# Attention block and 7x7 depthwise convolution on one core: how the rows for TensorE's share of the convolution are loaded, where a test of sums stands, and where the last additions go

## The chip, the cores and the metric

The kernel runs on one core of one Trainium2 chip. The metric is the device time of one execution in microseconds (us). A profile of one execution accompanies it; in it PE is TensorE, PEld its weight loads, DVE VectorE, ACT ScalarE, POOL GpSimd and SP SyncE. A "q" after an engine's name (SPq, ACTq) marks the engine's instruction queue where it issues a DMA or waits.

## The reference

The input `x` is (16, 384, 32, 32): 16 images of 384 channels and 32x32 positions, all float32.

```python
# _gn: normalised over 32 groups of 12 channels and all positions (mean, variance, eps 1e-5)
# layer 0
qkv  = einsum('bnc,oc->bno', tokens(_gn(x)), w_qkv)            # 8 heads of 48
attn = softmax(einsum('bhnd,bhmd->bhnm', q, k) * 48 ** -0.5)   # 1024 x 1024 per head
o    = einsum('bhnm,bhmd->bhnd', attn, v)
x    = x + einsum('bnc,oc->bno', o, w_proj) + b_proj
# layer 1
w_sym = (w + rot90(w, 1) + rot90(w, 2) + rot90(w, 3)) * 0.25   # one 7x7 filter per channel
x    = x + depthwise_conv(_gn(x), w_sym, stride 1, pad 3)
```

## The kernel before

The kernel goes through the images one after another. For image `b` it makes q, k and v, the scores and the attention (`s_step`, `av_step`), and the projection; TensorE does all of that, and ScalarE the exponentials between. Channels stand on the 128 partitions, so an image is three tiles of 128 channels by 1024 positions; `(b, k)` below is tile `k` of image `b`. The convolution of image `b - 1` runs on VectorE meanwhile, as a list of operations made by `fold_ops` and taken one at a time by `tap()`: sums and differences of a padded copy (`side`, L733), weighted sums of rows (`rows_e`, `rows_o`, L736 and L739), and additions to the output tile (L746). A planner decides at build time where each of these stands: it keeps two clocks of estimated times (`clock`, `vclock`), a heap `later` filled by `after(wait, cost, f)`, and `applies` for ScalarE's work. On the chip every engine then runs its list strictly in order, and semaphores are all that ties the lists together.

Three tiles at the end, `PE_TILES` = (14, 2), (15, 2) and (15, 1), have their convolution on TensorE instead. The last tile, (15, 0), stays with VectorE. The way of a TensorE tile is:

- `conv_begin` normalises it into `xn`, and `conv_store` (L895) writes that to a buffer `xd` in the chip's main memory, split by row parity into two planes per channel, each with a margin of zero rows.
- `conv_load` (L910) reads it back for half a tile (`a` = 0, 1) into a buffer `sh` of 128 partitions by 4 groups of 512 positions. A partition of `sh` stands for one channel of 16 and one of eight row shifts; a group is another 16 channels. The rows overlap, so each half tile comes to 1 MB.
- `conv_on_pe` (L941) multiplies `sh` with matrices made from the filter (`conv_matrices`, from `wsh` and `eye`, both filled by `conv_prepare`): 7 column shifts by 4 groups, 28 matrix products per half tile, each recorded as two. `pe_conv` holds the pieces to be done; `conv_piece` does one and calls `loads` for more rows.
- `conv_take` (L956) copies the sums out of PSUM on ScalarE, `conv_perm` (L965) sorts their rows on TensorE, and `conv_add` (L980) adds the result to the tile on VectorE and stores it (L981).

Main-memory loads that are issued by one engine wait in its list for earlier ones: the program has eight semaphores for the DMAs of SP and ACT together, and a DMA that takes a semaphore waits until that one's last DMA has landed.

The end of the program is written out by hand in `fast_finish` and `fast_end`: last projection, statistics of image 15 (`groups_on_pe`, from L325 to L357), then the tail. In it SP issues the stores, `late["tail"]` splits the row loads between SP and ACT, and a loop drains what is left. A safety test belongs there too: `check_vector` (L1363 to L1370) reduces the softmax sums, `check_tensor` (L1376 to L1379) adds the findings over the partitions and writes `again`, by which a slower exact version would be run. PSUM buffers are taken in turn from two pools.

```python
RI, CG = KS + 1, P // (KS + 1)      # 8 row shifts, 16 channels to a group
NG = P // CG                        # 8 groups in a tile, 4 in a half
PLANE = (H // 2 + PAD) * W          # 608 numbers: one row parity of one channel
```

Of the kernel before, what the change touches and what calls it, by code (L numbers as in the profile page):

```python
# [10 lines left out]
F32 = mybir.dt.float32  # L11
I32 = mybir.dt.int32
AF = mybir.ActivationFunctionType
ALU = mybir.AluOpType
AX = mybir.AxisListType

P = 128
# [28 lines left out]
def kernel(  # L46
# [25 lines left out]
    nc = tc.nc  # L72

    B, C, H, W = x.shape
    N = H * W
# [44 lines left out]
    def run(general):  # L120
        tag = "g" if general else "f"
        with ExitStack() as stack:
# [697 lines left out]

            def conv_end(b, k):

                (nc.scalar if b == B - 1 and not general else nc.gpsimd).dma_start(  # L823
                    out[b, k * P : (k + 1) * P].rearrange("p h w -> p (h w)"), x1s.pop((b, k))
                )

# [5 lines left out]
            RI, CG = KS + 1, P // (KS + 1)  # L832
            NG = P // CG
            PLANE = (H // 2 + PAD) * W

            def conv_prepare():

                w_d = dconv.tile([C, (KS + 2) * KS], F32, tag="w", name="w_d")
                zero = tpool.tile([P, N], F32, tag="t", name="zero")[:, 0 : 2 * W]
                nc.gpsimd.memset(zero, 0.0)  # L840
                w_rows = w_d.rearrange("(k p) t -> p k t", p=P)
                with nc.allow_non_contiguous_dma(reason="small, once"):
                    nc.gpsimd.dma_start(
                        w_rows[:, :, KS : (KS + 1) * KS], wsym.rearrange("p k i j -> p k (i j)")
                    )
                    none = zero[:, 0 : NK * KS].rearrange("p (k t) -> p k t", k=NK)
                    nc.gpsimd.dma_start(w_rows[:, :, 0:KS], none)
                    nc.gpsimd.dma_start(w_rows[:, :, (KS + 1) * KS :], none)
                    for n, k in enumerate(PE_K):
                        for i in range(RI):  # L850
                            nc.gpsimd.dma_start(
                                wsh[CG * i : CG * (i + 1), n].rearrange("p g t d -> p g (t d)"),
                                bass.AP(
                                    w_d.tensor,
                                    w_d.offset + (k * P * (KS + 2) + i) * KS,
                                    [[(KS + 2) * KS, CG], [CG * (KS + 2) * KS, NG], [1, 2 * KS]],
                                ),
                            )
                for bk in PE_TILES:
                    xd = dconv.tile([P, 2 * PLANE], F32, tag=f"x_{len(xds)}", name=f"xd_{len(xds)}")  # L860
                    xds[bk] = xd

                    for lo, n in ((0, 1), (H // 2 + 1, 2), (H // 2 + 3, 2), (2 * PLANE // W - 1, 1)):
                        nc.gpsimd.dma_start(xd[:, lo * W : (lo + n) * W], zero[:, 0 : n * W])
                for q in range(RI):
                    src = ident[:, CG * q : CG * (q + 1)]
                    if q == 0:
                        nc.gpsimd.tensor_copy(eye, src)
                    else:
                        nc.gpsimd.tensor_tensor(eye, eye, src, ALU.add)  # L870
                for row in range(2):
                    nc.gpsimd.tensor_copy(
                        perm[:, row].rearrange("p (g c) -> p g c", c=CG),
                        ident.rearrange("p (g t c) -> p t g c", t=2, c=CG)[:, 1 - row],
                    )
# [28 lines left out]
            def conv_load(b, k, a):  # L904

                t = qkpool.tile([P, 2, N], F32, tag="qk", name=f"sh_{b}_{k}_{a}")
                t = t.rearrange("p a n -> p (a n)").rearrange("p (g n) -> p g n", n=HALF)
                xd = xds[b, k]
                for i in range(RI):
                    (nc.scalar if late.get("tail") and i % 2 else nc.sync).dma_start(  # L910
                        t[CG * i : CG * (i + 1)],
                        bass.AP(
                            xd.tensor,
                            xd.offset
                            + a * NG // 2 * CG * 2 * PLANE
                            + (0 if i % 2 else PLANE)
                            + i // 2 * W,
                            [[2 * PLANE, CG], [CG * 2 * PLANE, NG // 2], [1, HALF]],
                        ),
                    )  # L920
                shs[b, k, a] = t
# [36 lines left out]
            def conv_perm(b, k, a):  # L958

                nonlocal clock  # L960
                if (b, k) not in pss:
                    pss[b, k] = psum(f"ps_rows_{b}_{k}")
                part = slice(64 * a, 64 * a + 64)
                for row in range(2):
                    nc.tensor.matmul(  # L965
                        pss[b, k][part, row, :],
                        lhsT=perm[:, row],
                        rhs=shs[b, k][:, a, :],
                        start=True,
                        stop=True,  # L970
                    )
                clock += 2.2
                if (b, k) == PE_TILES[-1]:
                    after(0.5, 1.3, lambda: conv_add(b, k, part, (nc.scalar, nc.sync)[a]))
                elif a == 1:
                    after(3.5 if b < B - 1 else 0.5, 1.3, lambda: conv_add(b, k, slice(0, P), nc.gpsimd))

            def conv_add(b, k, part, queue):
                dst = by_rows(x1s[b, k][part])
                nc.vector.tensor_tensor(dst, grids(pss[b, k][part]), dst, ALU.add)  # L980
                queue.dma_start(  # L981
                    out[b, k * P + part.start : k * P + part.stop].rearrange("p h w -> p (h w)"),
                    x1s[b, k][part],
                )
# [100 lines left out]
            def after(wait, cost, f):  # L1085

                nonlocal count
                count += 1
                heapq.heappush(later, (now() + wait, count, cost, f))
# [280 lines left out]
                nc.vector.memset(ones, 1.0)  # L1370
                lims.append((ones, lim))

            def check_tensor(pair):
                ones, lim = pair
                ps = psum("ps_again")
                nc.tensor.matmul(ps[0:1, 0, 0:2], lhsT=ones, rhs=lim, start=True, stop=True)  # L1376
                good = small.tile([1, 1], F32, tag="good", name="good")
                nc.vector.tensor_reduce(good, ps[0:1, 0, 0:2], AX.X, ALU.add)
                nc.vector.tensor_scalar(again, good, -1.0, 2.0 * P, ALU.mult, ALU.add)  # L1379
# [60 lines left out]
            def fast_finish(b):  # L1440
                nonlocal clock, vclock
                late["tail"] = b == B - 1

                for o in range(NK):
                    proj_part(b, o, 1, (0, 1))
                    if o < 2:
                        divide_at_once(o)
                    if o == 0:
                        tap()
                conv_piece()  # L1450
                for t in (2, 3):
                    for o in range(NK):
                        proj_part(b, o, 1, (t,))
                for o in range(NK):
                    half_done(b, o, 1)
                    if o == 0:
                        x1_stats[b].first_channels(x1s[b, o])
                clock += 2 * US_PROJ + 1.0
                vclock = clock + 2.5

            def fast_end(b):
                nonlocal clock, vclock
                assert not applies
                x1_stats[b].groups_on_pe(late["masks"], tap, lambda: conv_piece(False))
                conv_piece(False)
                x1_chains(b, x1_stats[b])
                clock = now()
                vclock = clock + 1.0
                after(0.0, 1.2, check_vector)
                heapq.heappop(applies)[-1]()  # L1470
                loads(2)
                clock += 3.0
                heapq.heappop(applies)[-1]()
                conv_rows()
                clock += 4.5

            def once(key, when):
                if when and key not in late:
# [63 lines left out]
            fast_end(B - 1)  # L1542
            while later or state["done"] < len(order) or active or pe_conv or perms:
                if pe_conv:
                    if pe_conv[0][0] == B - 1 and lims:
                        check_tensor(lims.pop())
                    conv_piece()
                elif perms:
                    conv_rows()
                else:  # L1550
                    clock = now() + 1.0
                act_slot(9.0)
                catch_up(clock)
# [51 lines left out]
```

## Time and profile before

| | us |
|---|---|
| median of 3 runs | 2870.86 (2870.76 to 2872.58) |
| the profiled execution, its own time | 2872.72 |
| its span, first to last instruction | 2870.9 |
| PE busy | 2832.4 (99%) |
| DVE busy | 2083.9 (73%) |
| ACT busy | 1649.1 (57%) |
| POOL busy | 250.6 (9%) |

The span is what the profile explains; 1.8 us of the execution's time lie around it. The shares are means over stages with different limits: the last 75 us of the span, after the statistics of image 15, have another pattern than the 2,795 us before. In a timeline row the first two numbers are the start from the span's beginning and the duration, "xN" is the number of instructions merged in the row, and the brackets hold the engine's idle time before it and what ended that. In the chain of waits a row is a piece of the chain that ended last.

### The profile page before, as it was taken

The page shows a single profiled execution, that of the slowest core. Times are in us where ns is not written, and L with a number is a line of the kernel's source. Part 1 is how long each engine was busy: PE and PEld are TensorE (multiplying, and loading weights), DVE is VectorE, ACT ScalarE, POOL GpSimd, SP SyncE. Part 2 cuts the span into 40 slices and gives each one's busy share as a digit, 9 for nine tenths or more (in the row PEclk, how much of TensorE's full clock was granted, in tenths as well). Part 3 has the DMA queues.
Part 4 walks back from the last instruction along what each step waited for, and adds up shares of the span by engine and source line. Part 5 has one row for each costly group of instructions (what it writes and reads, how often), then busy time and mean ns, then how long its engine had stood idle before and what let it go on. Part 6 is the DMA issues. An engine that isn't in the chain of part 4 may idle for free.

```text
span 2870.9 us, 46047 instructions
## 1 busy us (share of the span) xinstructions
PE 2832.4 (99%) x19342; PEld 1115.2 (39%) x19342; DVE 2083.9 (73%) x2257; ACT 1649.1 (57%) x1925; POOL 250.6 (9%) x410
## 2 busy tenths in 40 slices
PE   9999999999999999999999999999999999999995
PEld 5344343433434344343433434344343433434331
DVE  4502968959597695968959597695968959597776
ACT  2637647475674747647475674747647375674730
POOL 3201012210101001010010101001010010101000
PEclk9999999999999999999999999999999999999998
DMA  6612131211212112130211212112130211212215
GB/s 239 189 37 49 32 75 29 53 49 44 63 33 62 45 37 64 32 75 24 50 50 44 63 33 62 45 37 63 32 75 24 50 50 44 64 33 60 78 39 103
DMA packets 75657, 167.35 MB, mean 58 GB/s; under 512 B 31952, under 2 KB 34000, under 8 KB 73904
## 3 DMA queue, kind: packets, MB, share of 16 engines
q0 software_dynamic: 32400, 107.53, 14.3%
q1 hardware_dynamic: 41536, 54.16, 7.5%
q10 hardware_dynamic: 1504, 2.62, 0.6%
q8 instruction: 154, 2.52, 0.4%
q14 instruction: 63, 0.52, 0.1%
HBM read 117.09 MB, written 28.68 MB: 51 GB/s over the span
## 4 chain that ended last, share of the span: by engine, by line
PE 95%; DVE 3%; DMA 1%; issue 1%; ACT 0%; ACTq 0%; POOL 0%; SPq 0%; DVEq 0%; POOLq 0%
PE ps_s L518 30%; PE acc L538 30%; PE ps_qk L447 17%; PE ps_v L473 9%; PE ps_proj L599 8%; DVE x L746 1%; DVE rows_e L736 1%; DMA sh<-xd 1%; PE warm L1325 0%; DVE side L733 0%; DMA inv<-rec 0%; DMA inv<-inv 0%; DVE rows_o L736 0%; DVE x L736 0%; DVE x L980 0%
## 5 line engine op out<-in xcount | busy, mean ns | idle before, releaser
L526 ACT ACTIVATE e<-ps_s 128x1024 f32<-128x1024 f32 x1024 | 1021.2, 1030 | 448.1 <-PE ps_s L518 447.4
L538 PE MATMUL acc<-e,v 64*64 64x512 f32 x8192 | 1040.5, 588 | 0.6 <-ACT o L551 0.6
L518 PE MATMUL ps_s<-qk 48*64 48x512 f32 x8192 | 1040.8, 589 | 0.0
L733 DVE TENSOR_TENSOR side<-padded 128x1024 f32<-128x1024 f32 x270 | 329.0, 1219 | 345.5 <-ACT padded L704 345.5
L736 DVE SCALAR_TENSOR_TENSOR rows_e<-side,even,rows_e 128x1024 f32<-128x1024 f32 x405 | 509.6, 1274 | 85.6 <-ACT rows_e L715 84.0
L538 PEld LDWEIGHTS acc<-e,v 64*64 64x64 f32 x8192 | 308.8, 132 | 575.8 <-issue 574.2
L518 PEld LDWEIGHTS ps_s<-qk 48*64 48x64 f32 x8192 | 307.5, 132 | 577.4 <-issue 525.8
L447 PE MATMUL ps_qk<-x,wqk 128*128 128x512 f32 x1152 | 502.8, 595 | 0.0
L447 PEld LDWEIGHTS ps_qk<-x,wqk 128*128 128x128 f32 x1152 | 218.2, 191 | 278.0 <-issue 272.4
L746 DVE TENSOR_TENSOR x<-x,rows_o 128x992 f32<-128x992 f32 (+3 forms) x271 | 309.8, 1144 | 3.0
L746 DVE TENSOR_TENSOR x<-x,rows_e 128x992 f32<-128x992 f32 (+2 forms) x270 | 310.8, 1151 | 0.0
L454 ACT COPY qk<-ps_qk 128x1024 f32<-128x1024 f32 x96 | 97.2, 1012 | 319.4 <-PE ps_qk L447 319.4
L473 PE MATMUL ps_v<-wv,x 128*128 128x384 f32 x768 | 252.6, 486 | 0.0
L599 PE MATMUL ps_proj<-o,wp 128*128 128x512 f32 x540 | 234.2, 592 | 0.0
L493 ACT COPY v<-ps_v 64x384 f32<-64x384 f32 x256 | 121.4, 474 | 122.5 <-PE ps_v L473 120.0
L473 PEld LDWEIGHTS ps_v<-wv,x 128*128 128x128 f32 x768 | 145.9, 190 | 108.2 <-issue 14.3
L736 DVE SCALAR_TENSOR_TENSOR rows_o<-side,odd,rows_o 128x1024 f32<-128x1024 f32 x135 | 172.8, 1280 | 1.6
L736 DVE SCALAR_TENSOR_TENSOR x<-side,even,x 128x1024 f32<-128x1024 f32 x135 | 172.5, 1278 | 0.0
L823 POOL DMA_DIRECT2D out<-x x44 | 24.8, 563 | 1600.3 <-DVE x L746 1599.8
L715 ACT ACTIVATE rows_e<-padded,even 128x1024 f32<-128x1024 f32 x135 | 146.7, 1166 | 11.0 <-DMA sh<-xd 11.0
L599 PEld LDWEIGHTS ps_proj<-o,wp 128*128 128x128 f32 x540 | 102.6, 190 | 126.2 <-issue 117.4
L607 ACT ACTIVATE x<-ps_proj,bp 128x1024 f32<-128x1024 f32 x45 | 50.1, 1114 | 167.6 <-PE ps_proj L599 167.6
(145 smaller groups left out, 1013.1 us busy)
## 6 DMA issues: line engine op xcount, KB each, us to landing
x<-in_x POOLq DMA_DIRECT2D x90, 512.0 KB, 5.5
inv<-inv SPq DMA_DIRECT2D x126, 256.0 KB
out<-x POOLq DMA_DIRECT2D x46, 512.0 KB, 3.0
xs<-in_x POOLq DMA_DIRECT2D x42, 512.0 KB, 6.4
qk<-qk POOLq DMA_DIRECT2D x96, 128.0 KB, 4.1
o<-o SPq DMA_DIRECT2D x180, 32.0 KB
sh<-xd SPq DMA_DIRECT2D x32, 128.0 KB
x<-in_x SPq DMA_DIRECT2D x6, 512.0 KB
```

What stands on the lines that cost most here:

```text
L447: nc.tensor.matmul(ps[:, h, :], lhsT=wqk[:, k, s, t, :], rhs=xns[b][:, k, h * HALF : (h + 1) * HALF], start=(k == 0), stop=(k == NK - 1),)
L454: nc.scalar.copy(halves(qks[u][:, s, :]), ps)
L473: nc.tensor.matmul(ps[:, j, 0:C], lhsT=xns[b][:, k, t * P : (t + 1) * P], rhs=wv[:, k, :], start=(k == 0), stop=(k == NK - 1),)
L493: nc.scalar.copy(dst[:, :, 0 : HEADS // 2 * (D + 1)].rearrange("p k (h d) -> p k h d", d=D + 1)[:, :, :, 0:D], src.rearrange("p k (h d) -> ...
L518: nc.tensor.matmul(ps[64 * c : 64 * c + 64, a, :], lhsT=qk[r, 1, 64 * kb : 64 * kb + 64], rhs=qk[r, 0, h * HALF : (h + 1) * HALF], start=True,
L526: nc.scalar.activation(es[n], ps, AF.Exp, scale=SCALE)
L538: nc.tensor.matmul(accs[a][64 * j : 64 * j + 64, :], lhsT=v[rows, kb, c : c + 64], rhs=e[rows, j, :], start=(kb == 0), stop=(kb == 2 * NT ...
L599: nc.tensor.matmul(ps[:, h, :], lhsT=wp[:, t, o * P : (o + 1) * P], rhs=os_[b, t // 2][:, t % 2, h * HALF : (h + 1) * HALF], start=(t == 0 ...
L715: nc.scalar.activation(grid(rows_e[dy - 1]), padded_view(i), AF.Identity, scale=even[:, k, dy, 0:1],)
L733: vec.tensor_tensor(grid(sides[n]), padded_view(i, j), padded_view(i, -j), op)
L736: vec.scalar_tensor_tensor(dst, src, w, dst, ALU.mult, ALU.add)
L746: vec.tensor_tensor(dst, dst, src[:, lo + dy * W : hi + dy * W], op)
```

## The change

- **Row loads.** `conv_load` issues 4 DMAs per half tile, one per group, each to all 128 partitions of that group; before it was 8, one per row shift, each to 16 partitions and all four groups. The partitions are numbered with the channel outermost and the shift innermost. All are issued by SP. `wsh` and `eye` are filled in the same numbering by a new function `inputs`.
- **Test of the sums.** `check_vector` is called in `fast_finish`, ahead of the last part of the projection; `check_tensor` keeps only the matrix product and is called in the middle of the statistics, ahead of a convolution piece; the two small VectorE operations become `check_end`, called once the statistics are applied.
- **Additions.** Tiles (14, 2) and (15, 2) are no longer added by VectorE: ScalarE copies the sorted rows to a buffer `conv`, and POOL issues a DMA that adds the buffer to the tile, and then the store. The two half additions of (15, 1) are put 13.0 us of planner time later.
- **Order in `fast_end`.** The copies `conv_take` of (14, 2) come ahead of `rows_e`, `conv_perm` after it.

```diff
             def conv_end(b, k):
-                (nc.scalar if b == B - 1 and not general else nc.gpsimd).dma_start(
+                nc.gpsimd.dma_start(
...
+            def inputs(i):
+                first = (1 - i % 2) * RI // 2 + i // 2
+                return slice(first, first + (CG - 1) * RI + 1, RI)
             def conv_prepare():
...
-                                wsh[CG * i : CG * (i + 1), n].rearrange("p g t d -> p g (t d)"),
+                                wsh[inputs(i), n].rearrange("p g t d -> p g (t d)"),
...
-                    src = ident[:, CG * q : CG * (q + 1)]
+                    src = ident[:, inputs(q)]
...
             def conv_load(b, k, a):
...
-                for i in range(RI):
-                    (nc.scalar if late.get("tail") and i % 2 else nc.sync).dma_start(
-                        t[CG * i : CG * (i + 1)],
+                for i in range(NG // 2):
+                    nc.sync.dma_start(
+                        t[:, i],
                         bass.AP(
                             xd.tensor,
-                            xd.offset
-                            + a * NG // 2 * CG * 2 * PLANE
-                            + (0 if i % 2 else PLANE)
-                            + i // 2 * W,
-                            [[2 * PLANE, CG], [CG * 2 * PLANE, NG // 2], [1, HALF]],
+                            xd.offset + (a * NG // 2 + i) * CG * 2 * PLANE,
+                            [[PLANE, 2 * CG], [W, RI // 2], [1, HALF]],
                         ),
                     )
...
             def conv_perm(b, k, a):
...
                 if (b, k) == PE_TILES[-1]:
-                    after(0.5, 1.3, lambda: conv_add(b, k, part, (nc.scalar, nc.sync)[a]))
+                    after(13.0, 1.3, lambda: conv_add(b, k, part, (nc.scalar, nc.sync)[a]))
                 elif a == 1:
-                    after(3.5 if b < B - 1 else 0.5, 1.3, lambda: conv_add(b, k, slice(0, P), nc.gpsimd))
+                    t = tpool.tile([P, N], F32, tag="t", name=f"conv_{b}_{k}")
+                    nc.scalar.copy(by_rows(t), grids(pss.pop((b, k))))
+                    nc.gpsimd.dma_start(x1s[b, k], t, accum_op=ALU.add)
+                    conv_end(b, k)
...
-            def check_tensor(pair):
-                ones, lim = pair
+            def check_tensor():
+                ones, lim = lims.pop()
                 ps = psum("ps_again")
                 nc.tensor.matmul(ps[0:1, 0, 0:2], lhsT=ones, rhs=lim, start=True, stop=True)
+                lims.append(ps)
+
+            def check_end():
+                ps = lims.pop()
                 good = small.tile([1, 1], F32, tag="good", name="good")
...
             def fast_finish(b):
...
+                check_vector()
                 conv_piece()
...
             def fast_end(b):
...
-                x1_stats[b].groups_on_pe(late["masks"], tap, lambda: conv_piece(False))
+                x1_stats[b].groups_on_pe(
+                    late["masks"], tap, lambda: (check_tensor(), conv_piece(False))
+                )
                 conv_piece(False)
                 x1_chains(b, x1_stats[b])
                 clock = now()
                 vclock = clock + 1.0
-                after(0.0, 1.2, check_vector)
+                check_end()
                 heapq.heappop(applies)[-1]()
                 loads(2)
+                for p in perms:
+                    conv_take(*p)
+                heapq.heappop(applies)[-1]()
+                while perms:
+                    conv_perm(*perms.popleft())
                 clock += 3.0
-                heapq.heappop(applies)[-1]()
-                conv_rows()
-                clock += 4.5
...
-                    if pe_conv[0][0] == B - 1 and lims:
-                        check_tensor(lims.pop())
```

## The prediction

> **What bounds the kernel now.** I read the page's shares first. PE is busy for 99% of the span, so up to the end of the last projection nothing but TensorE's own work counts; none of that work is changed. The chain of waits over the last 75 us tells another story:
>
> ```profile
> 2797.27 0.81 DVE xn L363
> ...
> 2798.11 2.83 DMA xd<-xn
> ...
> 2802.47 7.83 DMA sh<-xd
> ...
> 2810.69 3.23 ACT rows_e L715 x3
> 2813.92 0.48 ACT rows L956
> ...
> 2814.53 4.08 PE ps_rows L965 x8
> ...
> 2818.63 1.23 DVE x L980
> ```
>
> The statistics are ready at 2797.2, and VectorE begins the convolution of (15, 0), the list that ends the program, only at 2819.8. Its first entry is the addition for (14, 2), which waits for PE's row sorting, which waits for ACT's copies, which stand behind row loads that ACT issues. ACT's timeline and the waits of this stretch show the queue:
>
> ```profile
> 2801.12 9.52 ACTq L910 DMA_DIRECT2D sh<-xd  x8
> 2810.69 3.23 ACT L715 ACTIVATE rows_e<-padded,even 128x1024 f32<-128x1024 f32 x3 [11.03 <-DMA sh<-xd]
> ```
> ```profile
> DVE x L980 <- PE ps_rows L965: 19.5, 1, 19.5
> PE ps_rows L965 <- ACT rows L956: 15.9, 3, 14.5
> ```
>
> ACT issues eight loads but is held 9.52 us, because it has to wait for earlier ones to land. Why they are slow is seen in a table of stretches (last columns: PE clock, DMA share, GB/s):
>
> ```profile
> 2799.00:2802.00 3.00, 1.05 (x12) 0.13 (x4) 0.12 (x2) 0.66 (x1) 0.00 (x0) 1.00 0.93 350
> 2812.00:2826.00 14.00, 11.47 (x82) 3.66 (x82) 7.33 (x9) 2.87 (x4) 0.59 (x1) 0.75 1.07 129
> ```
>
> The stores from 128 partitions move 350 GB/s at 0.93 busy; the loads to 16 partitions move 129 GB/s at full business. From 2819.8 to 2865.2 VectorE never stops. PE's row of work for (15, 2) and (15, 1) runs beside it:
>
> ```profile
> 2818.53 6.12 PE L941 MATMUL ps_conv<-sh,mat 128*32 128x512 f32 x56
> ...
> 2849.26 1.93 PE L965 MATMUL ps_rows<-rows,perm 128*64 128x512 f32 x4 [0.70 <-ACT rows L956]
> ```
>
> That is 32.7 us from 2818.53 to 2851.19, two waits of 0.7 for ACT's copies included. The last store is issued at 2865.20 and the span ends 5.7 us later. So the tail is: 22 us of waiting, 45.4 us of VectorE, 5.7 us of store.
>
> **What the Trainium skill says.** "SBUF — State Buffer", section "Door 1: The DMA port swizzle", states that the rate of a transfer follows the ports that its partitions reach: 104 GB/s measured for partitions 0 to 15, 328 for 0 to 127, at 1 MiB. The trace agrees in kind with 129 and 350; two queues that load different sixteens may explain why 129 is above 104. "DMA: Bandwidth & Descriptors", section "Issuing engines are not separate DMA queues", states that issuing from a second engine saves only the sequencer's time. In this trace it costs ACT 9.5 us of waiting.
>
> **Part by part.** Times are those of the profiled span.
>
> *Row loads.* In the tail 32 loads of 128 KB become 16 of 256 KB, all on SP, none on ACT: ACT loses three blocks of 9.5, 3.8 and 2.0 us. SP needs 0.30 to 0.64 us for an issue, so four take about 2 us and carry 1.05 MB, faster than the data flow; behind them on SP stand only the next loads and, far later, stores. The first can go at 2801.09 as before, since it waits for the store of (15, 2), landed at 2800.94. That store took 2.83 us for 0.52 MB, of which 1.5 is data at 350, so some 1.3 us pass before data flow (an estimate). At the skill's 328 GB/s, close to the trace's 350, half a tile takes 3.2 us: the first half of (15, 2) is in at 2801.1 + 1.3 + 3.2 = 2805.6, the other three at 2808.8, 2812 and 2815.2. PE wants them at 2812 or later, so they are hidden. The rate is the unknown here. From below it is the present 129 to 135 (all 4.2 MB by 2833), from above 350.
> For (14, 2), at 2715 to 2734, 16 issues on SP become 8, so VectorE's 8.9 us of idle time there, for reciprocals that SP sends behind the loads, shrinks. Worth nothing: PE is busy throughout, and VectorE later waits 3.4 us for PE anyway. `wsh` and `eye` keep their counts of 16 DMAs and 8 POOL operations, near 500 us, long before use: nothing, and some us of POOL's 91% idle time if not.
>
> *Test of the sums.* Seven operations (2797.99 to 2799.1, 1.1 us) go into the wait of 3.4 us for the last projection (VectorE free at 2783.1, PE done at 2786.5): nothing while that wait exceeds 1.1. The two small ones, 0.25 us, come ahead of the wait for `padded`, ACT's work until 2799.66: hidden in its 1.6 us. The matrix product (two records, 0.16 us each, overlapped) now stands between the two averages: plus 0.15 us, taken between 0 and 0.4.
>
> *Order at the start of the tail.* PE ends (14, 2) at 2800.05, 2800.2 with the line above. ACT, done with `padded`, copies at once (0.46 us apart), PE sorts rows from 2800.9 for 4.1 us, until 2805.0. `rows_e` follows on ACT, 3.2 us, ready at 2804.5; VectorE needs it at 2806.8. So PE begins (15, 2) at 2805.7, when the loads are in, and not at 2818.53; its clock, 0.50 from 2806 to 2818, should stay up.
>
> *VectorE.* It starts at 2799.8 with `side`. From 2819.86 to 2857.56, 37.7 us stand ahead of the place of the first half addition of (15, 1); minus the addition for (15, 2) (1.13), two halves now placed later (1.12 and 1.29) and the test (0.24), 33.9 remain: it is there at 2833.7. After it come 7.6 us of old work and two halves of 1.17: 9.95 us.
>
> *The two additions moved to ScalarE and POOL.* Two ACT copies of 128x1024, 1.0 us each by the nearest row (L454), two adding DMAs on POOL (0.88 us issue, 5.4 to landing, by L614) and two stores (0.56, 3.0). For (15, 2): sorted at 2828, copied at 2829.3, added at 2835.6, stored at 2839.2, some 10 us before VectorE ends. POOL has nothing else queued. ACT's second copy stands ahead of the copy for (15, 1), for which PE waits: 1.6 us beside 1.8 us of PE work, so 0.1 (0 to 0.4). If that cover were gone it would cost PE up to 1.6. The first copy runs from 2805.1 and delays nobody.
>
> *The wait that takes over.* In the instruction list of the changed kernel the first half addition waits for the last row sorting of PE, not for its own half; the second has no wait. So what is late next is PE: 2805.7 + 32.66 + 0.1 = 2838.5. VectorE stands from 2833.7 to 2838.5 with its remaining 9.95 us behind it, the final stores among what they release, then ends at 2848.5. With 5.7 of store the span is 2854.2, 16.7 below. The profiled execution took 2872.72, the median of the runs is 2870.86; the difference lies around the span and between runs, so I take 16.7 off the median: 2854.2.
>
> **The rivals.**
> 1. *The late addition does not bind*: the first half is released by its own sorting, at 2831.7. VectorE's own list then decides: 2833.7 + 9.95 + 5.7 = 2849.4. Against it stands the instruction list.
> 2. *The loads stay as slow as now*, limited by the reading of 2 KB pieces and not by partitions: at 135 GB/s the halves land 7.8 us apart, from 2810.2. PE then waits at each half tile and ends near 2845.2; 2845.2 + 9.95 + 5.7 = 2860.9. For it: no load of this kind and shape is in the trace. Against it: loads of weights at 2716 to 2718, in runs of 1.5 KB, show 362 to 392 GB/s.
> 3. *Slower: the reading collides.* A new load takes all its pieces from one block of 78 KB, each byte up to four times, by all 16 DMA engines at once; before they came from 16 channels in each of four blocks. At half the present rate, 66 GB/s, the last load lands at 2802.4 + 63.5 = 2866; PE needs 10.5 us from there, VectorE 9.95, the store 5.7: 2892. It decides below 99 GB/s, where the last load lands after 2844.7. Nothing in the profile speaks for it, but nothing measures it.
> 4. *No change*: something on ACT still holds VectorE for the 20 us. ACT has only 2.5 us of work ahead of `padded`, so hardly.
>
> **How the numbers follow.** The main case gets 0.68, the first rival 0.06, the second 0.16, the third 0.06, no change 0.04. A measurement of this kernel tells about 0.2%, 5.7 us, from no change. Main case, first and second rival all lie beyond it: faster 0.90, same 0.04, slower 0.06. The main case's own range is 2852 to 2858 (loads between 350 and 200 GB/s, the small unknowns at both ends). The range takes in the first rival at 2849.4 and the second at 2860.9.
>
> **What would show it.** Right: no ACTq row for `sh` in the tail; `side` starting near 2800; PE's (15, 2) near 2806; a stretch above 250 GB/s after 2802; a wait of about 5 us of VectorE for `ps_rows` before the first half addition, and none ahead of it; last store issued near 2848.5. Rival 1 shows as no such wait, rivals 2 and 3 as PE waiting for `sh` at each half tile with the DMA share near 1. An adding DMA or its store landing after 2849 would make the sum wrong at POOL.

## The result, and the profile after

| | before | after |
|---|---|---|
| median, us | 2871.67 (2870.76 to 2873.19, 5 runs) | 2858.36 (2856.75 to 2859.54, 5 runs) |
| profiled execution, its own time | 2872.72 | 2858.36 |
| its span | 2870.9 | 2856.6 |

After over before is 0.9953, with a 95% interval of 0.9938 to 0.9967: 13.3 us shorter by the medians, 14.3 by the spans. In these two profiles the whole difference is in the tail. VectorE begins the last scale of the statistics, `sc_x` on L357, at 2797.07 before and at 2797.13 after; from there to the end of the span it is 73.8 us before and 59.5 after. That `sc_x` stands at the same place is chance: after has its last projection done 1.6 us sooner (2784.93 against 2786.53), and its statistics take 1.7 us longer, which is taken up below. The distance from `sc_x` to the end, called the tail below, is used for all kernels, because `sc_x` wanders by several us between executions and the medians carry that.

In the changed kernel the line numbers are a few higher: row loads L916, TensorE's convolution L944, ACT's copies L959, row sorting L968, half additions L986, last stores L817. First the timeline of after (start, duration, engine, line; in brackets the idle time before and what ended it):

```profile
2799.76 1.23 DVE L733 TENSOR_TENSOR side<-padded 128x1024 f32<-128x1024 f32 x1 [1.39 <-ACT padded L704]
...
2800.91 2.33 PE L968 MATMUL ps_rows<-rows,perm 128*64 128x512 f32 x8 [0.80 <-ACT rows L959]
...
2801.10 12.56 SPq L916 DMA_DIRECT2D sh<-xd  x16
...
2804.18 1.67 PE L944 MATMUL ps_conv<-sh,mat 128*32 128x512 f32 x4 [0.95 <-DMA sh<-xd]
2806.41 1.04 PE L944 MATMUL ps_conv<-sh,mat 128*32 128x512 f32 x2 [0.56 <-DMA sh<-xd]
2807.70 7.53 PE L944 MATMUL ps_conv<-sh,mat 128*32 128x512 f32 x66 [0.24 <-DMA sh<-xd]
...
2831.28 1.93 PE L968 MATMUL ps_rows<-rows,perm 128*64 128x512 f32 x4
...
2838.11 1.93 PE L968 MATMUL ps_rows<-rows,perm 128*64 128x512 f32 x4 [0.70 <-ACT rows L959]
...
2840.08 1.22 DVE L986 TENSOR_TENSOR x<-ps_rows,x 64x1024 f32<-64x1024 f32 x1 [6.39 <-PE ps_rows L968]
...
2850.30 0.36 SPq L817 DMA_DIRECT2D out<-x  x1
```

VectorE begins `side` at 2799.76 where it was 2819.78. There is no row load on ACT's queue any more, and SP issues sixteen. PE needs all four loads of a half tile for its first column shift: it begins (15, 2) three times, each time waiting for the next load, and from 2807.70 on its only waits are two of 0.7 us for ACT's copies. VectorE arrives at the first half addition at 2840.08 - 6.39 = 2833.69 and then stands until PE's last sorting is done, although the sorting of its own half ended at 2833.2. The chain of waits of after says the same (start, duration, piece):

```profile
2803.01 4.65 DMA sh<-xd
...
2807.70 7.54 PE ps_conv L944 x59
...
2838.11 1.95 PE ps_rows L968 x4
...
2840.08 1.22 DVE x L986
...
2849.07 1.19 DVE x L746 x2
```

A load, then PE for 32 us, then VectorE for ten: ACT's queue has left the chain, and PE has taken its place. The table of stretches of after (last three columns: PE clock, DMA share, GB/s) has the rate of the loads:

```profile
2799.00:2802.00 3.00, 2.20 (x17) 0.66 (x11) 2.24 (x2) 2.55 (x4) 0.00 (x0) 1.00 0.92 350
2802.00:2804.00 2.00, 1.23 (x5) 0.14 (x1) 2.00 (x3) 2.00 (x3) 0.00 (x0) 1.00 0.71 224
2804.00:2806.00 2.00, 1.67 (x4) 0.28 (x4) 2.00 (x3) 1.30 (x2) 0.40 (x1) 1.00 0.86 258
2806.00:2808.00 2.00, 1.35 (x6) 0.29 (x10) 2.00 (x3) 0.00 (x0) 0.51 (x1) 1.00 1.04 301
```

From 2802 the loads flow at 224 to 301 GB/s (an adding DMA of POOL is in the last of these stretches), against 129 at full business before, and PE's clock stays at 1.00.

### The profile page after: what moved, and what is told of

It is laid out like the page before. It is cut to its first block, busy times and chain, and to the rows that moved or that the text cites. A ratio compares the mean times of both kernels' runs of the same rounds, so it can differ in the third digit from the quotient of the medians.

```text
span 2856.6 us, 45997 instructions
## 1 busy us (share of the span) xinstructions
PE 2833.9 (99%) x19342; PEld 1118.3 (39%) x19342; DVE 2081.7 (73%) x2255; ACT 1651.9 (58%) x1927; POOL 252.9 (9%) x412
## 4 chain that ended last, share of the span: by engine, by line
PE 98%; issue 1%; DVE 1%; DMA 0%; SPq 0%; POOL 0%; ACT 0%; POOLq 0%
PE ps_s L518 31%; PE acc L538 31%; PE ps_qk L447 17%; PE ps_v L473 9%; PE ps_proj L599 8%; PE ps_conv L944 1%; PE warm L1331 0%; DVE x L746 0%; PE ps_rows L968 0%; PE ps_proj_last L643 0%; DMA sh<-xd 0%; PE ps_st_x L335 0%; DMA xd<-xn 0%; DVE x L986 0%; DVE rows_o L736 0%
## 5 line engine op out<-in xcount | busy, mean ns | idle before, releaser
L473 PEld LDWEIGHTS ps_v<-wv,x 128*128 128x128 f32 x768 | 145.9, 190 | 108.2 <-issue 14.3
```

The costliest lines, as they stand in the source:

```text
L473: nc.tensor.matmul(ps[:, j, 0:C], lhsT=xns[b][:, k, t * P : (t + 1) * P], rhs=wv[:, k, :], start=(k == 0), stop=(k == NK - 1),)
```

## The experiments

Every kernel was timed against the kernel before on the same chip; the table comes first, the reasons after it. "sc_x" is when the last scale is ready in the profiled execution, "tail" the span minus that. A "yes" in the last column means that TensorE's clock fell inside the statistics, which is taken up further down.

| kernel | median, us | over before, 95% | span | sc_x | tail | clock fell |
|---|---|---|---|---|---|---|
| before | 2871.67 | | 2870.9 | 2797.07 | 73.8 | no |
| after | 2858.36 | 0.9953 (0.9938 to 0.9967) | 2856.6 | 2797.13 | 59.5 | yes |
| e1 loads only | 2859.76 | 0.9957 (0.9943 to 0.9970) | 2855.4 | 2792.58 | 62.8 | no |
| e2 old loads | 2867.56 | 0.9979 (0.9969 to 0.9989) | 2867.4 | 2798.85 | 68.6 | no |
| e5 old loads, SP alone | 2865.12 | 0.9980 (0.9972 to 0.9988) | 2862.6 | 2795.09 | 67.5 | no |
| e3 half additions last | 2852.58 | 0.9931 (0.9917 to 0.9945) | 2849.4 | 2796.07 | 53.3 | yes |
| e4 additions on VectorE | 2859.50 | 0.9949 (0.9937 to 0.9962) | 2859.8 | 2797.47 | 62.3 | yes |
| e10 as e3, additions on VectorE | 2860.87 | 0.9960 (0.9946 to 0.9974) | 2859.4 | 2797.49 | 61.9 | yes |
| e6 product late | 2858.69 | 0.9952 (0.9940 to 0.9965) | 2861.1 | 2800.39 | 60.7 | yes |
| e7 two queues | 2855.57 | 0.9947 (0.9934 to 0.9960) | 2853.7 | 2794.19 | 59.5 | no |
| e9 two queues, after the copies | 2857.11 | 0.9950 (0.9937 to 0.9964) | 2863.0 | 2798.70 | 64.3 | yes |
| e11 SP and POOL | 2858.27 | 0.9954 (0.9937 to 0.9971) | 2858.7 | 2799.86 | 58.8 | yes |
| e8 all three | 2851.94 | 0.9930 (0.9917 to 0.9943) | 2851.7 | 2798.41 | 53.3 | yes |

The medians of before beside these lay between 2869.96 and 2872.79, so two rows are compared by their distance from the before beside them, or by the tails; a tail is that of one execution.

### Which part carries it: the loads alone, and all but the loads

e1 is the kernel before with nothing but the new `conv_load` and the numbering in `wsh` and `eye`:

```diff
+                for i in range(NG // 2):
+                    nc.sync.dma_start(
+                        t[:, i],
...
+                            [[PLANE, 2 * CG], [W, RI // 2], [1, HALF]],
```

> The kernel before with the new row loads alone (four loads to 128 partitions per half tile, all on SP, and the numbering that goes with them). Theory: the loads are nearly the whole gain. ACT is then free after padded at 2799.7, makes rows_e until 2803 and the copies until 2804, PE sorts until 2806, VectorE adds (14, 2) and begins side at 2807.2 instead of 2819.8; its old list of 45.4 us has no further wait, since the first half addition is here released by its own half; end 2852.6, span about 2858.7, so 12 of the 14.3 us. Rival (the additions moved off VectorE and the test of the sums carry half of it): span 2863 or more. Rival (loads bring nothing by themselves): 2870.

e2 is the changed kernel with these lines as they were before:

```diff
-                for i in range(NG // 2):
-                    nc.sync.dma_start(
-                        t[:, i],
+                for i in range(RI):
+                    (nc.scalar if late.get("tail") and i % 2 else nc.sync).dma_start(
+                        t[CG * i : CG * (i + 1)],
```

> The changed kernel with the old row loads (eight per half tile to 16 partitions, every second one on ACT in the tail). Theory: ACT is held about 9.5 us again before the copies and rows_e; VectorE starts side at 2799.8 but waits some 6 us for rows_e; PE begins (15, 2) near 2814, sorts the last rows near 2847, and the first half addition waits for that: span about 2863, seven to eight us above the changed kernel. Rival (the loads are worth little once VectorE no longer begins with an addition): span within 2 us of the changed kernel's 2856.6.

e1 came to 2859.76, 1.4 us above the changed kernel: the loads alone bring nearly the whole gain. Without them 5.1 us of it are left (2872.61 - 2867.56); by the tails e2 is 9.1 us above the changed kernel, more than the seven to eight expected. The two don't add up to the whole, 12.9 and 5.1 against 13.3, because both parts take away waits of the same stretch, in which VectorE stands behind ACT. In the timeline of e1 ACT is free, but the copies for (14, 2) still stand behind `rows_e`:

```profile
2798.34 1.05 ACT L958 COPY rows<-ps_conv 128x512 f32<-128x512 f32 x2
...
2799.05 4.07 PE L967 MATMUL ps_rows<-rows,perm 128*64 128x512 f32 x8 [3.49 <-ACT rows L958]
...
2803.16 1.22 DVE L982 TENSOR_TENSOR x<-ps_rows,x 128x1024 f32<-128x1024 f32 x1 [8.53 <-PE ps_rows L967]
```

VectorE starts its list 11.7 us after `sc_x` (2804.30 - 2792.58), not 22.7 as before: 11.0 us sooner, and the tail is 11.0 us shorter (73.8 to 62.8). Here VectorE's own list decides to the end. The changed kernel starts it at 2.6 us, nine sooner again, and gets only 3.3 of them, since VectorE then waits 6.4 for PE.

### Rate or queue: the old loads on SP alone

Two costs of the old loads were tangled: 16 partitions at a time, and ACT held in its queue. e5 is e2 with the second taken away.

```diff
-                    (nc.scalar if late.get("tail") and i % 2 else nc.sync).dma_start(
+                    nc.sync.dma_start(
                         t[CG * i : CG * (i + 1)],
```

> The changed kernel with the loads of 16 partitions back, but all 16 of a tile on SP and none on ACT. It parts the two costs of the old loads: their rate, and ACT being held for 9.5 us. Theory (both count): ACT is free, so VectorE's convolution of (15, 0) starts near 2799.8 as in the changed kernel, but PE waits at each half tile of (15, 2) and (15, 1), the halves 7.8 us apart at 135 GB/s, the last row sorting ends near 2845, and the span is 2861 to 2863, about 5 us above the changed kernel's 2856.6 and 5 below the 2867.4 of the old loads on two engines. If one queue loads at the skill's 104 GB/s for 16 partitions, the halves come 10 us apart, PE ends near 2853 and the span is near 2870. Rival (only ACT's queue counted, the rate is hidden): the span stays at 2856 to 2858.

The timeline of e2, where ACT issues half of the loads:

```profile
2802.89 9.51 ACTq L916 DMA_DIRECT2D sh<-xd  x8
2812.44 1.07 ACT L962 COPY rows<-ps_conv 128x512 f32<-128x512 f32 x2 [11.00 <-DMA sh<-xd]
...
2817.14 7.54 PE L947 MATMUL ps_conv<-sh,mat 128*32 128x512 f32 x72
```

The timeline of e5, where ACT issues none:

```profile
2798.13 1.07 ACT L962 COPY rows<-ps_conv 128x512 f32<-128x512 f32 x2 [0.44 <-PE ps_conv L947]
...
2798.86 2.33 PE L971 MATMUL ps_rows<-rows,perm 128*64 128x512 f32 x8 [0.80 <-ACT rows L962]
2809.21 7.91 PE L947 MATMUL ps_conv<-sh,mat 128*32 128x512 f32 x56 [8.02 <-DMA sh<-xd]
...
2845.80 1.22 DVE L989 TENSOR_TENSOR x<-ps_rows,x 64x1024 f32<-64x1024 f32 x1 [14.14 <-PE ps_rows L971]
```

And a stretch of e5 that is mostly these loads (an adding DMA of POOL is issued within it):

```profile
2802.00:2808.00 6.00, 0.00 (x0) 0.00 (x0) 6.00 (x6) 1.26 (x2) 0.91 (x1) 0.87 1.07 134
```

In e5 ACT copies 3.0 us after `sc_x`, as in the changed kernel, and VectorE starts `side` at 2.6 as well. It does not help: PE stands 8.02 us for its rows, which arrive at 134 GB/s with the DMA engines full, and VectorE stands 14.14 us for PE. The tail is 8.0 us longer than the changed kernel's, where five were expected; putting half of the loads on ACT adds 1.0 more (68.55 against 67.51). The medians, each against its before, give 5.6 and 2.6 us for the two. So with the additions arranged as in the changed kernel the rate is the larger part of the price. In e2 PE begins (15, 2) 4.2 us later than in e5 (18.3 against 14.1 after `sc_x`), but then finds rows that came meanwhile, and the last sorting ends only 1.7 later (52.4 against 50.7). Three to nine us after the first issue one queue of 16-partition loads moved 132 to 135 GB/s in stretches of 2 us (e5), and the two queues of before 148 to 164; later the two moved 119 to 135. So it does not take two queues to get above 104, which the prediction had thought possible. The expectation's second case, an estimate from the 104 GB/s that the Trainium skill gives for partitions 0 to 15 at 1 MiB ("SBUF — State Buffer", section "Door 1: The DMA port swizzle"), did not come: with several loads to different sixteens in flight more was reached here. That such loads are far behind loads to all partitions holds.

### Where the late additions stand

e3 moves the two half additions of (15, 1) past all other work of VectorE:

```diff
-                    after(13.0, 1.3, lambda: conv_add(b, k, part, (nc.scalar, nc.sync)[a]))
+                    after(40.0, 1.3, lambda: conv_add(b, k, part, (nc.scalar, nc.sync)[a]))
```

> The changed kernel with the two half additions of (15, 1) at the very end of VectorE's list (40.0 us of planner time instead of 13.0). Theory: the 6.4 us in which VectorE stood for the last row sorting disappear, because it does its last seven operations (7.6 us) in that time: (15, 0) ends near 2841.3, the additions follow until 2843.8, and the span is 2849.5 to 2850.5, six to seven us below the changed kernel. Rival (the end of PE and what follows it bound the span whatever VectorE's order): the store of the second half, 256 KB from 64 partitions, lands as late after the additions as now, and the span falls by less than 2 us.

The timeline of e3:

```profile
2837.07 1.93 PE L968 MATMUL ps_rows<-rows,perm 128*64 128x512 f32 x4 [0.71 <-ACT rows L959]
...
2840.16 2.47 DVE L986 TENSOR_TENSOR x<-ps_rows,x 64x1024 f32<-64x1024 f32 x2
...
2842.65 0.59 SPq L987 DMA_DIRECT2D out<-x  x1
```

PE's last sorting ends at 2839.0, VectorE comes to the additions at 2840.16, and no wait stands before them. The tail is 53.3, 6.2 us less than the changed kernel's: the stall of 6.4 us cost nearly its whole length. With a median of 2852.58 it is a version that beats both kernels.

e4 takes the changed kernel and puts the additions for (14, 2) and (15, 2) back on VectorE:

```diff
-                    t = tpool.tile([P, N], F32, tag="t", name=f"conv_{b}_{k}")
-                    nc.scalar.copy(by_rows(t), grids(pss.pop((b, k))))
-                    nc.gpsimd.dma_start(x1s[b, k], t, accum_op=ALU.add)
-                    conv_end(b, k)
+                    after(3.5 if b < B - 1 else 0.5, 1.3, lambda: conv_add(b, k, slice(0, P), nc.gpsimd))
```

> The changed kernel with the additions for (14, 2) and (15, 2) on VectorE again (no copies on ACT, no adding DMAs). Theory: they are worth nothing here: VectorE adds (14, 2) first, near 2803.3, which costs 3.5 us of waiting and 1.1 of work, and (15, 2) later for 1.1 us; it then reaches the first half addition near 2839.5 and still waits for PE at 2840: span within 1 us of 2856.6, perhaps 0.5 below it because ACT and the DMA queues have less to do. Rival (VectorE's list bounds the end): 5 us more, 2862.

Its median is 1.1 us above the changed kernel's, less than either kernel's own spread. The timeline of e4:

```profile
2807.53 1.22 DVE L733 TENSOR_TENSOR side<-padded 128x1024 f32<-128x1024 f32 x1
...
2845.98 1.21 DVE L983 TENSOR_TENSOR x<-ps_rows,x 64x1024 f32<-64x1024 f32 x1
...
2851.86 1.23 DVE L983 TENSOR_TENSOR x<-ps_rows,x 64x1024 f32<-64x1024 f32 x1
```

VectorE starts `side` 10.1 us after `sc_x`, 7.4 later than in the changed kernel, and so comes late to the half additions: neither has a wait. The edit also moved them in VectorE's list, since the planner sets their place by its clock: the first stands three operations later than in the changed kernel, and the second at the very end. So e4 is not the changed kernel's order with two additions more; the extra work fills the stall that VectorE had anyway, and its own list decides to the end. The tail is 2.8 longer, and in this execution PE's half clock had stretched the last pieces of (14, 2) from 4.26 to 7.02 us, by the same 2.8. To see what the move is worth where there is no stall to fill, e10 makes the edit of e4 on e3:

> The two half additions of (15, 1) at the very end of VectorE's list, as in the run of the additions moved alone, and the whole additions for (14, 2) and (15, 2) back on VectorE. In the changed kernel VectorE stood 6.4 us for TensorE, so these additions cost there nothing or little. Theory (with the half additions last VectorE has no such wait, and now its own list is the end): VectorE waits for TensorE's sorting of (14, 2) before it begins (15, 0), 4.5 us later than at 2.6 us after sc_x, and does 2.3 us more work: the span ends 58 to 60 us after sc_x where the additions at the end alone took 53.3, and the median is 2857 to 2860. Rival (the moved additions never count): 53.3 and 2852.6 again.

The timeline of e10:

```profile
2806.15 1.23 DVE L983 TENSOR_TENSOR x<-ps_rows,x 128x1024 f32<-128x1024 f32 x1 [7.42 <-PE ps_rows L968]
2807.30 1.22 DVE L733 TENSOR_TENSOR side<-padded 128x1024 f32<-128x1024 f32 x1
```

Tail 61.9, median 2860.87, against 53.3 and 2852.58. VectorE begins `side` 9.8 us after `sc_x`, 7.2 later than in e3. With 1.2 for the addition of (15, 2) later in the list and a wait of 0.6 ahead of it, VectorE ends 9.0 us later than in e3, and the tail is 8.6 us longer. The half clock has 2.5 us of that (6.78 us for the pieces of (14, 2) instead of 4.26); about 6 are the additions. e4 and e10 differ in the place of the first half addition alone, and their tails by 0.4. So taking the additions off VectorE is worth about 6 us where the half additions stand last (e10 against e3), and about nothing between e4 and the changed kernel, which lets VectorE stand for PE instead.

### Does the product in the statistics cost anything?

In the profile of after VectorE waits 4.54 us for the second average, before 2.88. The only new thing on PE there is the product of the sums' test. e6 takes it out:

```diff
-                x1_stats[b].groups_on_pe(
-                    late["masks"], tap, lambda: (check_tensor(), conv_piece(False))
-                )
+                x1_stats[b].groups_on_pe(late["masks"], tap, lambda: conv_piece(False))
...
-                check_end()
...
+                    if pe_conv[0][0] == B - 1 and "tested" not in late:
+                        late["tested"] = True
+                        check_tensor()
+                        after(25.0, 0.3, check_end)
```

> The changed kernel with only the matrix product of the test of the sums, and the two small operations that read it, moved out of the last statistics: the product stands before TensorE's work for (15, 2), the reading some 15 us later. In the profile of the changed kernel the wait of VectorE for the second average took 4.54 us, in the kernel before 2.88, with TensorE's clock at 0.50 in that stretch. Theory (the product between the two averages brings it): 2.9 us here, and a span 1.5 us shorter. Rival (TensorE's clock falls there by chance): 2.9 or 4.5 us, whatever the product does, and a median within 1 us of the changed kernel's.

The timeline of e6, without the product:

```profile
2793.61 2.49 PE L944 MATMUL ps_conv<-sh,mat 128*32 128x512 f32 x16
2796.03 3.15 PE L335 MATMUL ps_st_x<-d_x,wv 128*128 128x1 f32 x14
...
2799.21 0.16 DVE L354 TENSOR_SCALAR d_x<-ps_st_x 128x3 f32<-128x3 f32 x1 [4.95 <-PE ps_st_x L335]
```

The timeline of e7, with it:

```profile
2789.50 1.83 PE L944 MATMUL ps_conv<-sh,mat 128*32 128x512 f32 x14
2791.26 1.72 PE L335 MATMUL ps_st_x<-d_x,wv 128*128 128x1 f32 x14
...
2793.02 0.16 DVE L354 TENSOR_SCALAR d_x<-ps_st_x 128x3 f32<-128x3 f32 x1 [2.89 <-PE ps_st_x L335]
```

And a stretch of e6 that lies within its second average, with the PE clock in the third column from the end:

```profile
2796.00:2798.00 2.00, 2.00 (x14) 1.97 (x10) 0.00 (x0) 0.00 (x0) 0.00 (x0) 0.50 0.00 0
```

The slow stretch is there without the product (e6, and e8 below) and absent with it (e7, e2, e5), so the product is neither needed for it nor enough: at the granted clock of 0.50 the average takes 3.15 us where it takes 1.72. With the full clock the product costs 0.01 us (waits of 2.89 and 2.88). What lowers the clock is open. It fell in nine of the fourteen profiles, in none of the two with the test in its old place; two are too few to say that this matters, and PE's rows up to there are the same in e6 and before. It lengthens the wait by 1.3 to 2.4 us and, where it lasts, the pieces of (14, 2) by up to 2.9.

### Can the first half tile come sooner?

PE began (15, 2) later than expected, and SP spends 0.6 us on an issue. Three kernels spread the four loads of that first half:

```diff
-                    nc.sync.dma_start(
+                    (nc.scalar if late.get("tail") and (b, k, a) == (B - 1, NK - 1, 0) and i % 2 else nc.sync).dma_start(
```

> The changed kernel with the four loads of the first half of (15, 2) issued by SP and ACT in turn. Theory (SP's issues of 0.6 us each keep the first half from starting): the half lands 1 to 1.5 us earlier, TensorE begins (15, 2) near 2806 and its last row sorting ends near 2838.7, the wait of VectorE before the first half addition falls from 6.4 to about 5 us, and the span is near 2855.3. ACT's copies come 1.2 to 2 us later, which TensorE can bear until 2805.5. Rival (the data flow limits, not the issue): TensorE begins at 2807.4 and the span stays within 0.4 us of 2856.6.

e7 has the tail of the changed kernel, 59.5, and its timeline shows why:

```profile
2798.23 1.47 ACTq L916 DMA_DIRECT2D sh<-xd  x2
2799.74 1.07 ACT L959 COPY rows<-ps_conv 128x512 f32<-128x512 f32 x2 [2.96 <-issue]
...
2800.47 4.07 PE L968 MATMUL ps_rows<-rows,perm 128*64 128x512 f32 x8 [3.30 <-ACT rows L959]
2804.47 8.45 PE L944 MATMUL ps_conv<-sh,mat 128*32 128x512 f32 x72
```

PE no longer waits for rows, but ACT's two loads hold the copies for 2.96 us, and after 3.30 us without work PE sorts at half the speed, 4.07 us instead of 2.33. It begins (15, 2) 10.28 us after `sc_x`, and its last sorting ends 43.5 us after it (2837.73), where the changed kernel's ends after 42.9. That the tails are equal all the same is the last store's doing, 5.7 us here and 6.3 there. The wait has changed its place, no more. The median is 2.8 us lower than the changed kernel's with overlapping ranges; the profile has no shorter tail to explain that, only a clock that did not fall, 1.7 us.

e9 is e7 with ACT's loads behind the copies, and was profiled twice:

```diff
-                loads(2)
                 for p in perms:
                     conv_take(*p)
+                loads(2)
```

> The changed kernel with the first half of (15, 2) loaded by SP and ACT in turn, and ACT's two loads placed behind its copies for (14, 2), which they held for 2.96 us where they stood ahead of them. Theory (the issue on SP alone costs TensorE 1.7 us, and the two queues lost this gain only by ACT's order): from the end of the statistics (the last scale, sc_x) the copies run 3 us later as in the changed kernel, TensorE begins (15, 2) 8.3 to 9 us after sc_x where the changed kernel and the two queues both took 10.3, the last row sorting ends 41.5 us after sc_x (42.9), and the span ends 58 us after it (59.5). Rival (the flow of data, not the issue, sets the first half): 10.3 and 59.5 again.

> The same kernel as that with ACT's two loads behind its copies, profiled once more: in the first profile TensorE's clock stood at 0.50 before its copies and again in (15, 2), so it could not tell. With a clock near 1.00: TensorE begins (15, 2) 8.3 to 9 us after sc_x if the issue on SP alone is the cost, 10.3 if it is not.

Neither profile could tell. In both the clock had fallen and stretched the pieces of (14, 2) to 6.9 and 7.1 us; the copies came late, ACT's loads behind them at 2804.6 and 2804.1, and PE waited 2.8 and 2.3 us for rows: tails of 64.3 and 62.2 (the second profile: span 2860.2, the execution's own time 2862.01). What they do show is that loads behind the copies share the copies' lateness.

e11 is e7 with POOL in place of ACT:

```diff
-                    (nc.scalar if late.get("tail") and
+                    (nc.gpsimd if late.get("tail") and
```

> The changed kernel with the first half of (15, 2) issued by SP and POOL in turn, so that ACT is not touched. POOL has nothing to do there until its adding DMA 4.5 us later. Theory (SP's four issues of 0.6 us keep the first half from flowing): the last piece of the half is in by 5 us after the first issue, where the changed kernel took 6.3, TensorE begins (15, 2) 8.3 to 9.3 us after sc_x instead of 10.3, and the span ends 58 to 58.5 us after sc_x instead of 59.5. Rival (the flow, or a POOL issue slower than SP's): 10.3 or later, 59.5 or more.

The timeline of e11:

```profile
2804.30 1.18 POOL L916 DMA_DIRECT2D sh<-xd  x2 [4.47 <-DMA xd<-xn]
...
2810.39 7.53 PE L944 MATMUL ps_conv<-sh,mat 128*32 128x512 f32 x66 [0.29 <-DMA sh<-xd]
```

PE runs freely 10.5 us after `sc_x` (10.6 in the changed kernel), 6.6 us after the first issue in both. The rival holds in its number: a second issuer brought PE nothing. Whether the flow of data is the limit, or POOL's two loads came in no sooner than SP's would have, this run does not part. It agrees with the Trainium skill, "DMA: Bandwidth & Descriptors", section "Issuing engines are not separate DMA queues": a second issuer saves the sequencer's time only.

e8 joins e3, the two queues of e7 and the late product of e6:

> The two half additions of (15, 1) at the very end of VectorE's list, the first half of (15, 2) loaded by SP and ACT in turn, and the product of the test before TensorE's work for (15, 2). With the additions at the end VectorE never waits for TensorE, so the earlier loads should bring nothing beyond the additions: a span of 2848 to 2850 and a median within 1.5 us of the 2852.6 of the additions moved alone. If TensorE's end still counts there, 1 to 2 us less.

Its tail is 53.3, that of e3, and its median 2851.94 against 2852.58: no difference, as expected. Where VectorE's list decides, PE's earlier start is worth nothing. e3 has the same gain with one number changed.

## Why the prediction was right, and where its sum was off

- **What bounded the kernel**: right. VectorE stood behind PE, PE behind ACT's copies, and these behind the row loads; with the loads changed alone (e1) VectorE starts 11.0 us sooner and the tail is 11.0 us shorter, one less than expected.
- **Which of the two costs of the loads**: the text gave the 20 us of VectorE's late start to ACT's queue and kept the rate as what PE would meet next. e5 and e2 show the second to be the larger in the changed order, 8.0 us against 1.0 by the tails and 5.6 against 2.6 by the medians. Its own second rival had this as 6.7 us (2860.9 - 2854.2), by the same mechanism.
- **VectorE**: right. Start 2799.8 (2799.76), first half addition reached at 2833.7 (2833.69). The 33.9 us between them were worked out; that the times themselves agree to the digit is luck, since `sc_x` itself lay between 2792.58 and 2800.39 in the kernels here.
- **The wait that takes over**: right. The first half addition waits for PE's last sorting, 6.4 us and not 4.8; e3 takes the wait away and the tail falls by 6.2. The first rival, that it would not bind, is out.
- **PE's start of (15, 2)**: the step that was mis-sized. Two terms were wrong. Sorting (14, 2) took 2.33 us, not 4.1, and ended at 2803.2, not 2805.0: the 4.1 came from a row of before in which PE had idled for 14.5 us, and after a wait of 0.80 it runs at full clock. The rows came later: the half was in at 2807.7, not 2805.6. The estimate had 328 GB/s from 1.3 us after the first issue; measured were 224, 258 and 301, while the loads of the next half and an adding DMA for (14, 2) flowed too. PE needs both, so the later one counts, and the sorting's gain went into waiting for rows: 2840.06 - 32.66 = 2807.4 for PE's start instead of 2805.7, and the last sorting 1.56 us later (2840.06 instead of 2838.5).
- **The rest of the sum**: VectorE's remaining work took 10.2 us, not 9.95, and the last store 6.3, not 5.7 (5.7 to 6.8 in the kernels here). 1.56 + 0.24 + 0.6 = 2.4 us, which is the whole distance between the predicted span of 2854.2 and the measured 2856.6. The median lies 4.2 us above the predicted one, and 0.4 above the main case's own range of 2852 to 2858. The other 1.8 us are the time around the span: the 16.7 were taken off the median of 2870.86 and not off the profiled execution's 2872.72, so that the predicted time came out no longer than the predicted span.
- **The test of the sums**: 0.15 us expected for the product, 0.01 found at full clock; the 1.66 us seen in the profile of after are a fallen clock (e6). On VectorE the test was hidden as said, a wait of 2.95 us being left after it.
- **The additions moved off VectorE**: their own times were near (that for (15, 2) ready to store at 2835.9, expected 2835.6). That for (14, 2) took 7.9 us to land beside the loads, against 5.4 expected, and nobody waited for it. The text did not say that the moves are worth about nothing once the wait takes over, to which e4 points; e10 shows them worth 6 us where it does not.
- **The third rival**, a collision in reading, did not occur: the new loads are nowhere below 224 GB/s in the three stretches shown.

## What to carry to other kernels

When a load feeds a chain, look at its rate in a table of stretches beside a transfer of another shape: 129 GB/s at full business beside 350 was the larger part of the story, and freeing ACT's queue alone (e5) left 8.0 us of it. After a change, put the work that waits for the last producer at the end of its engine's list: one number there (e3) gave 6 us, nearly half as much again as the change itself, and until it was done, taking two additions off VectorE was worth about nothing. Compare tails from a common event, not spans, when the event itself wanders by more than the effect: `sc_x` lay between 2792.58 and 2800.39.

## What was not expected of the hardware

- TensorE's granted clock fell to 0.50 within the statistics in nine of fourteen profiles, though PE had idled only 0.8 us there, and not in the other five; in six of the nine a column average took 3.15 us instead of 1.72. Its cause is open.
- The speed of the row sorting of (14, 2) goes with PE's wait ahead of it: 2.33 us after 0.80, 4.07 after 3.30 (e7) and after 3.49 (e1). In e8, after 1.86, it was 2.33. No run shows where between 1.86 and 3.30 it turns.
- In the changed kernel an adding DMA of 512 KB issued by POOL took 7.9 us from the end of its issue until its store could go where row loads were in flight, and 4.1 us where none were.
- 16-partition loads from one queue moved 132 to 135 GB/s (e5). Two queues moved 148 to 164 at the same distance from the first issue and 119 to 135 later (before).
